# Decoder kernel: local attention's second rotation product in its own buffer and ahead of the sum of squares, with a new order of the front and cross-attention norms on ACT

## Chip, cores and metric

The kernel runs as one program on one core of a Trainium2 chip. The metric is the device time of one execution in microseconds (us). "Before" was run three times. One more execution was profiled; all times inside the kernel come from that one and count from its first instruction. Engines are called PE (matrix multiply), DVE (vector), ACT (scalar, activations), POOL (GpSimd) and SP (which here only issues DMAs).

## What is computed

The reference is a decoder of two layers, each with an attention part, a cross-attention part and a feed-forward part, on x of shape (4, 512, 128), with a layernorm behind every part. Three parts matter here.

The first part of layer 0 is a selective scan (Mamba):

```python
xn = rmsnorm(x, norm_w)
x_part, z = split(xn @ in_proj_w.T)
u = silu(conv(x_part, conv_w) + conv_b)         # causal, 4 taps
dt, Bm, Cm = split(u @ x_proj_w.T)
delta = softplus(dt @ dt_proj_w.T + dt_proj_b)
h[t] = exp(delta[t] * A) * h[t-1] + delta[t] * Bm[t] * u[t]   # 16 states
y[t] = sum(h[t] * Cm[t]) + u[t] * D
out = (y * silu(z)) @ out_proj_w.T + x
```

The second part of layer 0 is cross attention over 32 context rows with 16 heads: `xn = layernorm(x) * gamma + beta`, scores, softmax, values, an output projection, a gate `tanh(gate)`, the residual, a layernorm.

The last part of layer 1 is a local transformer of two layers (8 heads of 64, windows of 64 rows that look one window back):

```python
h = shift_token(x)
q, k, v = split(h @ wqkv)
q = l2norm(q) * q_scale ; k = l2norm(k) * k_scale
q = q * cos * scale + rotate_half(q) * sin * scale     # k likewise, with / scale
x = x + local_attention(q, k, v) @ wo
h = layernorm(shift_token(x)) * lg + lb
a, g = split(h @ w1 + b1)
x = x + (a * gelu(g)) @ w2 + b2
```

## The kernel before, in words

Everything is one program; x is kept as 16 tiles of 128 rows (4 batches of 4 tiles). Each engine runs its own instructions in the order in which the program has them. Inside a `tc.manual_schedule()` block that order is the one in which the code emits them; between such blocks the tool that builds the program may interleave. So the order on an engine is written out by hand, as lists of functions ("around", "feed", "first", "ahead", "aside").

**The front** (L355 to L400) brings batch 0 of the scan to the point where the scan can start. `squares_(b)` squares the rows of a batch on ACT and sums them on DVE into `inv`; `inverses` raises them to the power -0.5 on POOL. Batch 0 is normed, transposed (`by_features`), projected (`pi`), and convolved: half of the channels on DVE (L370, L372), the other half as matmuls with the taps multiplied into the weights (`convolved`). Two Silu on ACT give `u`. `double` computes `px` and its two copies, `xdt` in float32 and `stk` in bfloat16. `rests` and `parts` split what bfloat16 leaves over into two further bfloat16 parts of `stk` (rows 32 to 63 and 64 to 95), which the scan's matmuls broadcast. `gates` makes the gate's pre-activation, with Silu into `sz`. `steps_`, `corrected`, `reduced`, `logarithms`, `deltas`, `products` compute softplus from Abs, Relu, Exp, 1 + e, a correction, and Ln, and then `delta` and `du = delta * u`.

**The scan** (L563 to L598) has 64 steps (4 batches of 16 states). In each, `rows` broadcasts a row of B and of C by matmuls, `decay` makes `dA` on ACT (three steps ahead), `scan` multiplies `pb` by `du` and scans on DVE, and multiplies by C on POOL; `collect` sums on PE. What the next batch needs is spread over the steps ("ahead"); `gates_next` at step 5 applies Silu to `u` and `sz` of the next batch.

**Cross attention** (L971 to L1095) runs 16 tiles in two half stages, `tile_a` and `tile_b`; parts of the mixture of experts that follows are put between them ("aside"). `stats_x` takes mean and variance of a tile of the next batch (DVE) and its power -0.5 (POOL, `rpow` in `stats`). `norm_x` norms that tile on DVE (L985) and transposes it; with the batch's fourth tile ACT writes `xT`, which `score` of the next batch needs. `result` makes the residual sum r and its statistics, `norm_r` norms it on DVE (L1036).

**Local attention** (L1392 to L1866) runs 32 tiles i (2 layers of 16), each in two iterations g = 2i and 2i + 1. PSUM buffers: `pqk` (one, two banks), `psc`, `pa` (one), and `pt`, a ring of three that all transposes, `pv`, `po` and `pff` share. The functions around the change:
- `project_qk(i)`: q and k of tile i into `pqk`.
- `squares(i)`: ACT squares `pqk` into the SBUF buffer "sq", of which there is one.
- `norms(i)`: DVE sums "sq" (L1439) and takes the maximum with 1e-24 (L1440), 128x16.
- `rotated_a(i)`: DVE, `ta = pqk * cos` (L1446).
- `halves(i)`: DVE, `tb = rotate_half(pqk) * sin`, two instructions (L1453). `tb` also lies in the buffer "sq". It is the last reader of `pqk`.
- `halves_added(i)`: POOL, `ta += tb` (L1459). `lengths(i)`: POOL, power -0.5 of the sums. `scaled(i)`: POOL, `ta *= rn` (L1467).
- `turn_k(i)`, `turn_q(i)`: PE transposes of ta into `pt`; `kT` is copied by DVE (L1488), `qT` by ACT.
- `values(g)`: PE; then DVE `rc` (L1543) and `at` (L1544). `output(i)`: PE `po`, DVE `xa = po + x` (L1562).
- `ff_gates`: two of its three products are written into the `pqk` buffer, the third into `pt`. `ff_hidden`: DVE `ge` (L1614). `ff_stats`: mean and variance, four tiles at once, with a 128x4 addition (L179).

Where two tiles are in work, "around" says what is emitted when; for odd iterations:

```python
[[(turn_out, -1), (rotated_a, 3)], [(norms, 3), (rotated_b, 3)], [(project_v, 2), (output, -1)]]
```

The first tiles (0 to 2) have an order of their own ("first"), which calls norms, rotated_a, halves.

Of the kernel before, what the change touches and what calls it, by code (L numbers as in the profile page):

```python
# [19 lines left out]
P = 128  # L20
# [37 lines left out]
def decoder_kernel(ctx: ExitStack, tc: tile.TileContext, a: dict):  # L58
# [178 lines left out]
    with ExitStack() as ph:  # L237
# [77 lines left out]
            G.tensor_tensor(stk[64:96, b, :], left[64:96], mid[64:96], ALU.subtract)  # L315


        def steps_(b, c, pd):
            mm(pd, w_dt[96:104, c * P:(c + 1) * P], xdts[b][96:104])
            t = fp.tile([P, T], F32, tag="e", name="e")  # L320
            v = fp.tile([P, T], F32, tag="v", name="v")
            S.activation(t, pd, AF.Abs, bias=vcol("dt_b", c))
            S.activation(v, pd, AF.Relu, bias=vcol("dt_b", c))
            S.activation(t, t, AF.Exp, scale=-1.0)
            w = fp.tile([P, T], F32, tag="w", name="w")
            S.activation(w, t, AF.Identity, bias=1.0)
            evs[b, c] = t, v, w

        def corrected(b, c):
# [25 lines left out]
        with tc.tile_pool(name="m1ps", bufs=1, space=PSUM) as ps, tc.manual_schedule():  # L355
            squares_(0)
            inverses(0, 1)
            xns[0] = fp.tile([P, NJ, D], F32, tag="e", name="xn")
            V.tensor_tensor(xns[0], x0[:, 0:NJ, :], inv[:, 0].unsqueeze(2).to_broadcast([P, NJ, D]), ALU.mult)
            by_features(0, ps.tile([P, NJ, P], F32, tag="pt", name="pt"))  # L360
            for c in range(2):
                G.tensor_tensor(w_tap[:, c], w_tap[:, c],
                                w_in[:, c * P:(c + 1) * P].unsqueeze(1).to_broadcast([P, 4, P]), ALU.mult)
            for b in range(1, B):
                squares_(b)

# [3 lines left out]
            V.tensor_scalar(acc, pi, vcol("conv_w", 7), vcol("conv_b", 1), ALU.mult, ALU.add)  # L370
            for k in range(1, 4):
                V.scalar_tensor_tensor(acc[:, k:], pi[:, 0:T - k], vcol("conv_w", 7 - k), acc[:, k:], ALU.mult, ALU.add)  # L372
            inverses(1, B)
            pi = ps.tile([P, T], F32, tag="pi0", name="pi")
            convolved(0, 0, pi, range(4))
            S.activation(u[:, 1, 0, :], acc, AF.Silu)
            S.activation(u[:, 0, 0, :], pi, AF.Silu, bias=vcol("conv_b", 0))
            double(0, ps.tile([104, T], F32, tag="px", name="px"))
            rests(0)
            pz = [ps.tile([P, T], F32, tag=f"pz{c}", name="pz") for c in range(2)]  # L380
            for c in range(2):
                gates(0, c, pz[c])
                S.activation(sz[:, c, 0, :], pz[c], AF.Silu)
            S.activation(gate, rcol("gate"), AF.Tanh)
            pct = ps.tile([P, P], F32, tag="pi1", name="pct")
            TE.transpose(pct, ctx_sb, ident)
            V.tensor_copy(ctxT, pct)
            a0 = _VEC["A_log"][0]
            S.activation(negA, vec[:, a0:a0 + 32], AF.Exp)
            V.tensor_scalar_mul(negA, negA, -1.0)  # L390
            V.tensor_scalar_mul(gb, rcol("b_out"), gate)
            for c in range(2):
                steps_(0, c, ps.tile([P, T], F32, tag=f"pd{c}", name="pd"))
                corrected(0, c)
                reduced(0, c, (G, V)[c])
            logarithms(0)
            for c, eng in ((0, G), (1, V)):
                deltas(0, c, eng)
                products(0, c, eng)
            parts(0)  # L400


        with tc.tile_pool(name="m2", bufs=3) as t2, \
# [19 lines left out]

            def decay(k):
                b, n = steps[k]
                for c in range(2):
                    S.activation(dAs[k % 4][:, c, c:T], delta[b % 2][:, c, c:T], AF.Exp,  # L427
                                 scale=negA[:, c * NST + n:c * NST + n + 1])

# [112 lines left out]
            def gates_next(b, c):  # L542
                pi = bank()
                gates(b, c, pi)
                S.copy(sz[:, c, b, :], pi)
                if c:
                    for t in (u, sz):
                        S.activation(t[:, :, b, :], t[:, :, b, :], AF.Silu)

            def double_next(b):  # L550
                double(b, bank()[0:104])
# [417 lines left out]
            store(hf, g)  # L969

    with tc.tile_pool(name="xa", bufs=3) as t1:  # L971
        xrs, mvs, ptx, xTs, scs, mxs, xes, rcs, prs, xpTs, rs_ = ({} for _ in range(11))

        def stats_x(i):
            mvs[i] = stats(x1[:, i, :])
            xrs[i] = t1.tile([P, D], F32, tag="xr", name="xr", bufs=8)
            G.tensor_tensor(xrs[i], x1[:, i, :], gb, ALU.add)

        def norm_x(i):
            b, j = divmod(i, NJ)  # L980
            if j == 0:
                ptx[b] = ps.tile([P, NJ, P], F32, tag="ph", name="ptx")
            mv, rs = mvs.pop(i)
            xn = t1.tile([P, D], F32, tag="xn", name="xn")
            V.tensor_scalar(xn, x1[:, i, :], mv[:, 0:1], rs, ALU.subtract, ALU.mult)  # L985
            TE.transpose(ptx[b][:, j, :], xn, ident)
            if j == NJ - 1:
                xTs[b] = t1.tile([P, T], F32, tag="xT", name="xT", bufs=2)
                S.activation(xTs[b], ptx.pop(b).rearrange("p j t -> p (j t)"), AF.Identity,
                             bias=vcol("ln_b"), scale=vcol("ln_g"))  # L990

        def score(i):
            b, j = divmod(i, NJ)
# [35 lines left out]
        def result(i):  # L1029
            r = rs_[i] = t1.tile([P, D], F32, tag="r", name="r")  # L1030
            V.scalar_tensor_tensor(r, pos_.pop(i), gate, xrs.pop(i), ALU.mult, ALU.add)
            mvs["r", i] = stats(r)

        def norm_r(i):
            mv, rs = mvs.pop(("r", i))
            V.tensor_scalar(x2[:, i, :], rs_.pop(i), mv[:, 0:1], rs, ALU.subtract, ALU.mult)  # L1036

        def tile_a(k):

# [352 lines left out]
    with tc.tile_pool(name="la_b", bufs=2) as bp, tc.tile_pool(name="la_t", bufs=2) as t1, \  # L1392
# [54 lines left out]

        def halves(i):
            src = pqks.pop(i).rearrange("p w (h d) -> p w h d", d=64)
            tb = tbs[i] = t1.tile([P, 2, 8, 64], F32, tag="sq", name="tb", bufs=1)  # L1450
            for hf in range(2):
                lo = slice(32 * hf, 32 * hf + 32)
                V.tensor_tensor(  # L1453
# [13 lines left out]
            G.tensor_tensor(ta, ta, rns.pop(i).unsqueeze(2).to_broadcast([P, 16, 64]), ALU.mult)  # L1467
# [297 lines left out]
        def x_norm(b):  # L1765
# [242 lines left out]
```

## Time and profile before

| what | value |
|---|---|
| three runs | 1251.81, 1258.32, 1264.30 us; median 1258.32 |
| the profiled execution | 1261.84 us |
| its span, first to last instruction | 1260.1 us |
| granted PE clock, mean of the span | 0.942 |
| front, to the start of the first scan instruction | 38.8 us |
| last scan instruction starts | 302.1 us |
| local attention: first `pqk`, last `ptq` | 829.9 us, 1208.7 us |

How to read it: a busy share over the whole span says little, because the stages have different limits. The windows give the busy time of each engine in a stretch. In timeline lines the columns are start (us), duration (us), engine, line, operation, out<-in with shapes, count; an idle time of the engine just before the instruction stands in brackets, with what ended it. Lines of merged instructions carry "x2", "x4" and so on. A line such as "PE pff L189: 7.3, 6" below a tile's name tells that this group waited for that tile for 7.3 us in 6 waits.

### The profile page before, as it was taken

To read this page: it belongs to the slowest core of one execution; us is meant where nothing else is said; L and a number is where in the kernel's file an instruction comes from. 1 tells how busy PE (TensorE), PEld (TensorE's weight loads), DVE (VectorE), ACT (ScalarE), POOL (GpSimd) and SP (SyncE) were. 2 spreads that over 40 slices of the span, in tenths; PEclk is the share of its full clock that TensorE was granted. 3 is DMA by queue.
4 is the path that set the end of the run, shared out by engine and by line. 5 is a ranking of instruction groups with operands and counts; after the bars stand their busy time and mean duration, and the time that the engine had idled before them with its cause. 6 is when DMAs were issued, how large, how long until landed. Compare 5 with 4: busy or idle time off the path is not lost.

```text
span 1260.1 us, 22102 instructions
## 1 busy us (share of the span) xinstructions
PE 1091.9 (87%) x8377; PEld 707.5 (56%) x8377; DVE 906.1 (72%) x1720; ACT 724.6 (58%) x1608; POOL 640.4 (51%) x525
## 2 busy tenths in 40 slices
PE   4879878786788899988899999787999999999995
PEld 1334433343365789955556566455666676666664
DVE  3889898897777465847856676687787677676663
ACT  5695968662243344545556566244676666666762
POOL 4568685865445242543110100356886675676641
PEclk9799989898788898989999999789999999999997
DMA  9000000000300522200000000001111011011100
GB/s 274 1 0 1 1 0 1 0 1 25 126 1 22 191 96 84 69 29 14 2 1 2 1 2 1 1 5 23 23 27 27 18 27 27 18 27 27 27 21 28
DMA packets 38739, 39.96 MB, mean 32 GB/s; under 512 B 7544, under 2 KB 29833, under 8 KB 38153
## 3 DMA queue, kind: packets, MB, share of 16 engines
q1 hardware_dynamic: 36041, 32.73, 9.2%
q0 software_dynamic: 2048, 4.20, 1.1%
q10 hardware_dynamic: 544, 1.62, 0.4%
q8 instruction: 66, 1.08, 0.3%
q14 instruction: 40, 0.33, 0.1%
HBM read 20.80 MB, written 9.18 MB: 24 GB/s over the span
## 4 chain that ended last, share of the span: by engine, by line
PE 46%; DVE 20%; issue 3%; ACT 3%; POOL 2%; DMA 2%; DVEq 0%; ACTq 0%; SPq 0%; POOLq 0%
PE psc L189 10%; PE pqk L189 4%; PE pa L189 4%; PE ptp L1260 3%; PE phg L189 3%; PE pff L189 3%; PE po L189 3%; PE pog L189 2%; PE pv L189 2%; DVE ss L1439 2%; DVE tb L1453 2%; DVE ta L1446 2%; PE pof L189 2%; PE pq L189 1%; DMA hn<-xa 1%
## 5 line engine op out<-in xcount | busy, mean ns | idle before, releaser
L440 POOL TENSOR_TENSOR h<-h,cb 128x1024 f32<-128x1024 f32 (+1 forms) x65 | 151.8, 2338 | 65.7 <-DVE h L435 50.4
L157 POOL TENSOR_TENSOR rs<-ve,cneg 128x1 f32<-128x1 f32 (+2 forms) x83 | 59.7, 719 | 224.3 <-DVE ve L166 189.1
L435 DVE TENSOR_TENSOR_SCAN h<-dA,pb 128x1024 f32<-128x1024 f32 x64 | 146.3, 2286 | 18.4 <-ACT dA L427 4.9
L1250 ACT ACTIVATE pe<-psc,nm 128x256 f32<-128x256 f32 (+1 forms) x256 | 93.3, 448 | 74.8 <-DVE nm L1243 74.4
L189 PE MATMUL y<-h,ident 128*128 128x512 f32 x256 | 127.1, 620 | 5.5 <-POOL h L440 4.8
L1459 POOL TENSOR_TENSOR ta<-ta,tb 128x1024 f32<-128x1024 f32 x32 | 75.4, 2357 | 102.8 <-DVE rc L1543 56.6
L1243 DVE TENSOR_REDUCE nm<-psc 128x4 f32<-128x1024 f32 (+1 forms) x64 | 69.8, 1090 | 54.4 <-PE psc L189 49.1
L157 POOL TENSOR_TENSOR rn<-ss,cneg 128x16 f32<-128x16 f32 x32 | 93.0, 2905 | 0.0
L1513 DVE TENSOR_REDUCE nm<-psc 128x4 f32<-128x512 f32 x64 | 44.0, 687 | 64.2 <-PE psc L189 60.0
L427 ACT ACTIVATE dA<-delta,negA 128x512 f32<-128x512 f32 (+1 forms) x128 | 85.3, 715 | 4.7 <-POOL delta L346 4.4
L189 PEld LDWEIGHTS y<-h,ident 128*128 128x128 f32 x256 | 49.5, 197 | 65.4 <-issue 46.5
L929 ACT ACTIVATE hTg<-phg,bias 128x128 f32<-128x128 f32 x184 | 52.6, 368 | 58.0 <-PE phg L189 57.3
L432 DVE TENSOR_TENSOR pb<-du,pb 128x1024 f32<-128x1024 f32 x64 | 77.5, 1211 | 2.3 <-PE pb L189 2.2
L1522 ACT ACTIVATE pe<-psc,nm 128x128 f32<-128x128 f32 x256 | 73.6, 380 | 5.1 <-DVE nm L1513 5.0
L1260 PE MATMUL ptp<-ident,pe 128*128 128x128 f32 x448 | 66.9, 285 | 5.2 <-ACT pT L1262 2.0
L189 PE MATMUL pb<-stk,sel 96*128 96x512 bf16 x128 | 41.4, 406 | 32.7 <-DVE h L435 15.5
L189 PE MATMUL pqk<-f_qkv,hT 128*128 128x512 f32 x128 | 65.2, 633 | 5.1 <-DVE tb L1453 5.1
L189 PE MATMUL psc<-kb,qk 64*128 64x256 f32 (+1 forms) x512 | 68.0, 386 | 0.0
L1260 PEld LDWEIGHTS ptp<-ident,pe 128*128 128x128 f32 x448 | 49.4, 143 | 23.2 <-issue 8.0
L1467 POOL TENSOR_TENSOR ta<-ta,rn 128x1024 f32<-128x1024 f32 x32 | 60.9, 1902 | 2.4
L1433 ACT ACTIVATE sq<-pqk 128x1024 f32<-128x1024 f32 x32 | 32.9, 1028 | 43.9 <-PE pqk L189 40.5
L189 PEld LDWEIGHTS <-sel 96*128 96x128 bf16 x192 | 18.9, 102 | 68.9 <-issue 41.7
(382 smaller groups left out, 2853.0 us busy)
## 6 DMA issues: line engine op xcount, KB each, us to landing
vh<-va SPq DMA_DIRECT2D x56, 130.0 KB
w<-in_e_w_dram SPq DMA_DIRECT2D x16, 256.0 KB
xs<-zero SPq DMA_DIRECT2D x2, 1472.0 KB
xg<-xs SPq DMA_DIRECT2D x10, 256.0 KB
ys<-yg SPq DMA_DIRECT2D x10, 256.0 KB
f_qkv<-in_f_qkv_dram SPq DMA_DIRECT2D x1, 1536.0 KB
x<-in_x_dram SPq DMA_DIRECT2D x4, 256.0 KB
w_kv<-in_w_kv_dram SPq DMA_DIRECT2D x1, 1024.0 KB
```

Of the source, the lines that this page charges most:

```text
L157: G.tensor_tensor(out, in_, cneg.to_broadcast([P, n]), ALU.pow)
L189: TE.matmul(out, lhsT=lhsT, rhs=rhs, start=start, stop=stop)
L427: S.activation(dAs[k % 4][:, c, c:T], delta[b % 2][:, c, c:T], AF.Exp, scale=negA[:, c * NST + n:c * NST + n + 1])
L432: V.tensor_tensor(pb, du[steps[k][0] % 2], pb, ALU.mult)
L435: V.tensor_tensor_scan(h.rearrange("p c t -> p (c t)"), dAs[k % 4].rearrange("p c t -> p (c t)"), pb.rearrange("p c t -> p (c t)"), 0.0, A ...
L440: G.tensor_tensor(h[:, c], h[:, c], cb.unsqueeze(1).to_broadcast([P, n, T]), ALU.mult)
L1243: V.tensor_reduce(nm, psc[:, :, 0:nk], AX.X, ALU.max, negate=True)
L1250: S.activation(pe[:, h, 0:nk], psc[:, h, 0:nk], AF.Exp, bias=nm[:, h:h + 1])
L1260: TE.transpose(ptp[:, h * nb + kk, :], pe[:, 2 * pr + h, kk * P:(kk + 1) * P], ident)
L1459: G.tensor_tensor(ta, ta, tbs.pop(i).rearrange("p w h d -> p (w h) d"), ALU.add)
L1467: G.tensor_tensor(ta, ta, rns.pop(i).unsqueeze(2).to_broadcast([P, 16, 64]), ALU.mult)
L1522: S.activation(pes[g][:, h, :], o[:, par, q, :], AF.Exp, bias=nm[:, k:k + 1])
```

## The change

In local attention `tb` gets a buffer of its own (one, 128x1024 float32), and in the odd iterations `norms` is emitted by `rotated_b`, behind `halves` and `halves_added`, instead of ahead of them. The order of tiles 0 to 2 ("first") stays.

In the front, the sums of squares of batches 1 to 3 are moved behind the convolution, between and behind the two Silu; `rests` and `parts` are written out and put right behind `double`, with their copies on DVE instead of ACT; Relu and 1 + e of batch 0 go from ACT to DVE; the gates of batch 0 come later and are only copied, by DVE, and their Silu is applied at scan step 5 with batch 1's. The first step's decay takes c = 1 first.

In cross attention, the statistics of a batch's four tiles are kept together, with one addition and one power for the four, and with two small POOL products that make `-mean * rs`; ACT norms the four tiles (`normal`, L202) in `tile_b` of the batch's second tile, and `turn_x` transposes them in `tile_a` of the third. `result` also makes `-mean * rs` with two POOL products, and `norm_r` is done by ACT.

```diff
-        def steps_(b, c, pd):
+        def steps_(b, c, pd, eng=None):
...
-            S.activation(v, pd, AF.Relu, bias=vcol("dt_b", c))
+            if eng:
+                eng.tensor_scalar(v, pd, vcol("dt_b", c), 0.0, ALU.add, ALU.max)
+            else:
+                S.activation(v, pd, AF.Relu, bias=vcol("dt_b", c))
...
-            S.activation(w, t, AF.Identity, bias=1.0)
+            if eng:
+                eng.tensor_scalar_add(w, t, 1.0)
+            else:
+                S.activation(w, t, AF.Identity, bias=1.0)
...
-            for b in range(1, B):
-                squares_(b)
...
-            inverses(1, B)
             pi = ps.tile([P, T], F32, tag="pi0", name="pi")
             convolved(0, 0, pi, range(4))
+            squares_(1)
             S.activation(u[:, 1, 0, :], acc, AF.Silu)
             S.activation(u[:, 0, 0, :], pi, AF.Silu, bias=vcol("conv_b", 0))
+            squares_(2)
+            squares_(3)
+            inverses(1, B)
             double(0, ps.tile([104, T], F32, tag="px", name="px"))
-            rests(0)
-            pz = [ps.tile([P, T], F32, tag=f"pz{c}", name="pz") for c in range(2)]
-            for c in range(2):
-                gates(0, c, pz[c])
-                S.activation(sz[:, c, 0, :], pz[c], AF.Silu)
+            left = fp.tile([P, T], F32, tag="left", name="left", bufs=1)[0:96]
+            V.tensor_tensor(left, xdts[0][0:96], stk[:, 0, :], ALU.subtract)
+            mid = fp.tile([96, T], BF16, tag="mid", name="mid", bufs=1)
+            V.tensor_copy(mid[64:96], left[64:96])
+            V.tensor_copy(stk[32:64, 0, :], left[32:64])
+            G.tensor_tensor(stk[64:96, 0, :], left[64:96], mid[64:96], ALU.subtract)
...
             for c in range(2):
-                steps_(0, c, ps.tile([P, T], F32, tag=f"pd{c}", name="pd"))
+                steps_(0, c, ps.tile([P, T], F32, tag=f"pd{c}", name="pd"), V)
                 corrected(0, c)
                 reduced(0, c, (G, V)[c])
+            for c in range(2):
+                pz = ps.tile([P, T], F32, tag=f"pz{c}", name="pz")
+                gates(0, c, pz)
+                V.tensor_copy(sz[:, c, 0, :], pz)
             logarithms(0)
...
-            parts(0)
...
-                for c in range(2):
+                for c in range(2) if k else (1, 0):
                     S.activation(dAs[k % 4][:, c, c:T], delta[b % 2][:, c, c:T], AF.Exp,
...
-                    for t in (u, sz):
-                        S.activation(t[:, :, b, :], t[:, :, b, :], AF.Silu)
+                    for t, i in ((u, b), (sz, b)) + ((sz, 0),) * (b == 1):
+                        S.activation(t[:, :, i, :], t[:, :, i, :], AF.Silu)
...
         def stats_x(i):
-            mvs[i] = stats(x1[:, i, :])
+            b, j = divmod(i, NJ)
+            if j == 0:
+                mvs[b] = sm.tile([P, NJ, 2], F32, tag="mv4", name="mv4")
+            st = sm.tile([P, 6], F32, tag="st", name="st")
+            V.bn_stats(st, x1[:, i, :])
+            V.bn_aggr(mvs[b][:, j, :], st)
...
             if j == NJ - 1:
+                ve = sm.tile([P, NJ], F32, tag="ve4", name="ve4")
+                V.tensor_tensor(ve, mvs[b][:, :, 1], eps.to_broadcast([P, NJ]), ALU.add)
+                rs = sm.tile([P, NJ], F32, tag="rs4", name="rs4")
+                rpow(rs, ve, NJ)
+                mvs[b] = mvs[b], rs, x1[:, b * NJ:(b + 1) * NJ, :], shifts(mvs[b], rs)
+
+        def norm_x(b):
+            xns_[b] = t1.tile([P, NJ, D], F32, tag="xn", name="xn", bufs=1)
+            normal(xns_[b], *mvs.pop(b))
+
+        def turn_x(b):
+            pt = ps.tile([P, NJ, P], F32, tag="ph", name="ptx")
+            xn = xns_.pop(b)
+            for j in range(NJ):
+                TE.transpose(pt[:, j, :], xn[:, j, :], ident)
+            xTs[b] = t1.tile([P, T], F32, tag="xT", name="xT", bufs=2)
+            S.activation(xTs[b], pt.rearrange("p j t -> p (j t)"), AF.Identity, bias=vcol("ln_b"), scale=vcol("ln_g"))
...
-            mvs["r", i] = stats(r)
+            mv, rs = stats(r)
+            mr = sm.tile([P, 1], F32, tag="mr1", name="mr1")
+            G.tensor_tensor(mr, mv[:, 0:1], rs, ALU.mult)
+            G.tensor_tensor(mr, mr, cminus, ALU.mult)
+            mvs["r", i] = mr, rs
 
         def norm_r(i):
-            mv, rs = mvs.pop(("r", i))
-            V.tensor_scalar(x2[:, i, :], rs_.pop(i), mv[:, 0:1], rs, ALU.subtract, ALU.mult)
+            mr, rs = mvs.pop(("r", i))
+            S.activation(x2[:, i, :], rs_.pop(i), AF.Identity, bias=mr, scale=rs)
...
+                if k % NJ == 2:
+                    turn_x(nxt // NJ)
...
-                for j in ((), (0, 1), (2, 3), ())[k % NJ]:
-                    norm_x(nxt + j)
+                if k % NJ == 1:
+                    norm_x(nxt // NJ)
...
-            tb = tbs[i] = t1.tile([P, 2, 8, 64], F32, tag="sq", name="tb", bufs=1)
+            tb = tbs[i] = t1.tile([P, 2, 8, 64], F32, tag="tb", name="tb", bufs=1)
...
-            for f in (halves, halves_added, lengths, scaled):
+            for f in (halves, halves_added, norms, lengths, scaled):
...
-                  [[(turn_out, -1), (rotated_a, 3)], [(norms, 3), (rotated_b, 3)], [(project_v, 2), (output, -1)]]]
+                  [[(turn_out, -1), (rotated_a, 3)], [(rotated_b, 3)], [(project_v, 2), (output, -1)]]]
```

More of the change, by code (lines that the diff above doesn't have):

```diff
@@ L971, in decoder_kernel @@
     with tc.tile_pool(name="xa", bufs=3) as t1:
-        xrs, mvs, ptx, xTs, scs, mxs, xes, rcs, prs, xpTs, rs_ = ({} for _ in range(11))
+        xrs, mvs, xns_, xTs, scs, mxs, xes, rcs, prs, xpTs, rs_ = ({} for _ in range(11))
         def stats_x(i):
-            mvs[i] = stats(x1[:, i, :])
+            b, j = divmod(i, NJ)
[4 more added lines that the diff above has]
+            V.bn_aggr(mvs[b][:, j, :], st)
             xrs[i] = t1.tile([P, D], F32, tag="xr", name="xr", bufs=8)
             G.tensor_tensor(xrs[i], x1[:, i, :], gb, ALU.add)
[L979 to L986, printed above, removed]
-            if j == NJ - 1:
-                xTs[b] = t1.tile([P, T], F32, tag="xT", name="xT", bufs=2)
-                S.activation(xTs[b], ptx.pop(b).rearrange("p j t -> p (j t)"), AF.Identity,
-                             bias=vcol("ln_b"), scale=vcol("ln_g"))
+            if j == NJ - 1:
+                ve = sm.tile([P, NJ], F32, tag="ve4", name="ve4")
[13 more added lines that the diff above has]
+            S.activation(xTs[b], pt.rearrange("p j t -> p (j t)"), AF.Identity, bias=vcol("ln_b"), scale=vcol("ln_g"))
         def score(i):
```

## The prediction

> **What bounds the kernel now.** I read the page's busy table and chain first, then windows by stage, then the timelines of the three stages that the change touches.
>
> ```profile
> PE 1091.9 (87%) x8377; PEld 707.5 (56%) x8377; DVE 906.1 (72%) x1720; ACT 724.6 (58%) x1608; POOL 640.4 (51%) x525
> ...
> PE 46%; DVE 20%; issue 3%; ACT 3%; POOL 2%; DMA 2%; DVEq 0%; ACTq 0%; SPq 0%; POOLq 0%
> ```
> ```profile
> 64.00:330.00 266.00, 217.74 (x682) 102.16 (x680) 231.78 (x219) 176.13 (x315) 182.79 (x113) 0.93 0.05 18
> ...
> 960.00:1040.00 80.00, 77.91 (x821) 53.04 (x821) 57.84 (x120) 50.20 (x116) 55.21 (x31) 1.00 0.11 25
> ```
> The columns after the length are PE, PEld, DVE, ACT, POOL, then clock, DMA share, GB/s. The scan (64 to 330) belongs to DVE, 87% busy. Local attention (830 to 1230) belongs to PE, 97% busy: a wait there costs its full length. One tile of it, DVE and PE:
>
> ```profile
> 1016.58 1.21 DVE L1446 TENSOR_TENSOR ta<-pqk,tab 128x1024 f32<-128x1024 f32 x1
> 1017.71 1.21 DVE L1439 TENSOR_REDUCE ss<-sq 128x16 f32<-128x1024 f32 x1
> 1018.95 0.18 DVE L1440 TENSOR_SCALAR ss<-ss 128x16 f32<-128x16 f32 x1
> 1019.04 1.28 DVE L1453 TENSOR_TENSOR tb<-pqk,tab 128x512 f32<-128x512 f32 x2
> 1020.24 0.17 DVE L1543 RECIPROCAL rc<-pa 128x4 f32<-128x4 f32 x1
> 1020.44 0.42 DVE L1544 TENSOR_TENSOR at<-pa,rc 128x256 f32<-128x256 f32 x1
> 1020.78 0.28 DVE L1562 TENSOR_TENSOR xa<-po,x 128x128 f32<-128x128 f32 x1
> ```
> ```profile
> 1020.51 0.60 PE L1486 MATMUL ptk<-ident,ta 128*128 128x128 f32 x4
> 1021.12 0.66 PE L1477 MATMUL ptq<-ident,ta 128*128 128x128 f32 x4
> ```
> DVE works without a gap from ta to xa. `xa` reads `po`, whose PSUM buffer `ptq` takes three `pt` tiles later; xa ends at 1021.06 and ptq follows 0.06 later. Setting every xa against its next ptq weight load in the trace, 21 of 29 pairs have this distance of 0.05; the others have 0.71, 1.09, or 3.6 and more. So DVE and PE are tied in most tiles, and a DVE delay in front of xa goes straight into the time.
>
> ```profile
> 947.33 2.84 PE L189 MATMUL pff<-hnT,f_w 128*128 128x512 f32 x6 [1.22 <-DVE tb L1453]
> ```
> ```profile
>   PE pff L189: 7.3, 6
> ```
> Here PE waits for tb, which holds the `pqk` buffer: 7.3 us in six waits. This wait is what tb ahead of ss removes.
>
> ```profile
> 848.82 1.85 DVE L1440 TENSOR_SCALAR ss<-ss 128x16 f32<-128x16 f32 x1
> ```
> ```profile
> 848.73 1.90 POOL L1467 TENSOR_TENSOR ta<-ta,rn 128x1024 f32<-128x1024 f32 x1
> ```
> The reader is to see that L1440, otherwise 0.17, ran until POOL's tensor_tensor was over (850.67 and 850.63). At 926.18 it took 0.91 beside another one. The 1.21 reduce ran undisturbed beside both.
>
> **Local attention, step by step.** tb takes the place of ss at 1017.71 and ends at 1018.99. POOL's ta+=tb starts 0.14 later (as at 1009.30 after 1009.16) and lasts 2.36, to 1021.49. DVE's ss runs beside it, to 1020.12; the maximum L1440 behind it meets the POOL operation that tb has just released. In the row above the maximum lost the rest of POOL's time, so it ends at 1021.52 and rc starts at 1021.43, not 1020.24: **1.19 later**. Queued behind it on DVE are (ge,) rc, at, xa, then nm and kT; PE's ptq waits for xa. Bounds: 0 (not held) to 1.19 (held to the end); I take 1.19, since the row is the same instruction against the same kind of partner. Price: 21 x 1.19 = 25.0, plus 0.48 and 0.10 for the distances 0.71 and 1.09: +25.6. In the tiles of the pff wait xa has 3.6 to 4.6 of slack, so the delay is free there, and the 7.3 are won (tb 1.38 earlier than a wait of 1.22; next is po's end at 946.1). The separate buffer lets sq go without waiting for ta+=tb: one such wait, 3.3 at 858.8, in the start; a PE wait of 2.0 follows it, of which I take 1.5. POOL's lengths and scaled move 1.2 earlier, to nobody's gain: no PE wait is on ta. Sum: 25.6 - 7.3 - 1.5 = **+16.8**. Bounds: -8.8 without the hold, +22 if neither gain comes.
>
> The Trainium skill, "SBUF — State Buffer", section "SBUF: two separate sides", calls this pair of ports an exclusive lock: whichever of a two-port DVE operation and a GpSimd operation starts first keeps it for its whole length. The rows agree for POOL's add and multiply. They differ for its power: L1440 took 0.17 at 888.87 inside a power of 887.97 to 888.98. By the rule the front's 2.28 power would also hold DVE's left for up to 2.1 and the estimate would be some 1.5 worse; by the rows it is not.
>
> **The front.**
> ```profile
> 14.65 0.80 DVE L370 TENSOR_SCALAR u<-pi,vec 128x512 f32<-128x512 f32 x1
> ...
> 36.32 1.01 PE L189 MATMUL pb<-stk,sel 96*128 96x512 bf16 x2 [11.53 <-POOL stk L315]
> ...
> 38.76 2.29 DVE L435 TENSOR_TENSOR_SCAN h<-dA,pb 128x1024 f32<-128x1024 f32 x1
> ```
> L370 stood behind the last sum of squares (14.04); its own input was ready at 11.66. It starts 2.9 earlier, but the second Silu needs the conv matmuls (11.45 + 4.95 = 16.40, against 18.37), so px comes 1.9 earlier and stk's cast ends near 20.2. From ACT go two Silu (1.2), two Relu (1.36), two Identity (1.26), two casts (1.24); DVE gets two relu (0.80 by L370), two adds (at most 0.69), two PSUM copies (0.69), two casts (at most 0.6). DVE then carries the front: left 0.69, casts 1.2, ctxT, negA, gb 0.75, relu, add, correction twice 4.3, reduced 0.69, copies 1.38, delta and du 1.38, about 10.4 in a row: du ends near 30.6. POOL tensor_tensors beside it (1.48, 1.26, 1.26) can hold it by 0 to 3.3; before, delta took 1.40 and du 1.64 instead of 0.69 beside POOL. I take 1.5: 32.1, pb's product 1.23, scan at 33.3, **5.5 earlier**. stk is ready near 24 and no longer last. ACT's first pair of decays, now c = 1 first, waits for DVE's delta (near 31.4) and ends 1.33 later, still hidden by du and pb's product. Square between the Silus could cost two table loads of 1.28; under Exp's table Square ran without one (956.19), so I take 0. The deferred Silu of sz comes back in the scan:
> ```profile
> 74.35 2.29 DVE L435 TENSOR_TENSOR_SCAN h<-dA,pb 128x1024 f32<-128x1024 f32 x1 [3.10 <-ACT cb L422]
> ```
> ACT is full in front of this wait, and a Silu of 1.04 (row at 67.44) lengthens it: +1.0. Sum **-4.5**; bounds -6.9 (no hold, Silu hidden) to 0 (loads, all holds, Silu). SP's and POOL's DMA order is untouched.
>
> **Cross attention, 314 to 413.**
> ```profile
> 330.41 2.07 PE L189 MATMUL sc<-Gm,xT 128*128 128x512 f32 x2 [0.87 <-ACT xT L989]
> ```
> ```profile
> 331.18 1.06 DVE L1036 TENSOR_SCALAR x<-r,mv,rs 128x128 f32<-128x128 f32 x1 [0.44 <-POOL rs L157]
> ```
> At each new batch sc waits for xT. The new chain from the last statistics: power 1.03, two small POOL products 0.56, four ACT norms 1.65, transposes 0.9, xT 0.78 = 4.9. From 321.84, 342.95, 362.95 that gives 326.8, 347.9, 367.9; PE's own work ends at 327.2, 346.2, 371.3; sc stood at 330.41, 349.85, 372.61: -3.2, -2.0, -1.3 = -6.5. Of the 16 norms that leave DVE five took 1.06 beside POOL; half of the 4.6 that the chain holds of them: -2. Against it 16 x 0.56 of POOL products before xpr, 9.0 at worst; rc comes 1.6 after ve and POOL needs 1.15, so mostly hidden: +2. ACT, about 40% busy here, covers 16 norms of 0.41; if it doesn't, xpT is late next. One 128x4 addition per batch in place of four small ones (0.14) is hidden behind POOL's power. Sum **-6.5**, bounds -11 to +3.
>
> **Sum:** 16.8 - 4.5 - 6.5 = +5.8. The profiled run took 1261.84 (span 1260.1 and 1.7 around it): 1267.6. It lies 3.5 over the median of three (1258.32); for a median I predict 1264.
>
> **Rivals.**
> *No hold* (the maximum slips past POOL, or PE's slack takes it): local attention -8.8, in all -19.8: 1238. For it: L1440 is small and normally 0.17. Against: both rows beside a tensor_tensor show the hold.
> *Slower: front and cross attention give nothing.* DVE inherits the front's work and meets POOL's tensor_tensors; ACT's norms wait for POOL products ahead of xpT. From sums over 0 to +2 together it decides: 16.8 + 1 = +18, 1276. For it: the 1.06, 1.40 and 1.64 rows. Against: PE's three visible waits for xT.
> *Slower: a second collision.* POOL's scaled (1.90), now 1.2 earlier, meets the statistics' 128x4 addition at 1023.3, eight times: 8 x 1.9 = 15, 1279. Against: kT and y, queued behind it, have over 1 us of slack by the rows.
> That tb isn't earlier at all I exclude: DVE's order is written out.
>
> **How the numbers follow.** About 1% (12.6 us) is what a measurement of this kernel can tell from no change. Forecast 0.49 (1254 to 1274; 0.41 within, 0.08 slower), no hold 0.18 (0.15 faster), nothing from front and cross 0.22 (0.19 slower), second collision 0.11 (0.10 slower). Faster 0.15, same 0.48, slower 0.37. The range goes down to 1240, past no hold with half of the other gains (-8.8 - 5.5: 1244 on the median), and up to 1282, past the two slower cases; left out are about half of no hold (0.09) and the far ends of the slower ones (0.09).
>
> **What would show it.** L1440's median near 1.4, not 0.17; PE's waits for tb gone and those for xa up from 4.9 to some 25 or more; first scan near 33; sc waiting less for xT. L1440 at 0.17 beside ta+=tb would make the prediction wrong, and so would a first scan after 37.

## The result, and the profile after

| | median | runs |
|---|---|---|
| before | 1261.19 us | 12, from 1251.81 to 1265.28 |
| changed | 1265.13 us | 12, from 1260.65 to 1271.09 |

The ratio is 1.005, with a 95% interval of 1.0026 to 1.0073. Measured a second time (after_again, below), against its own runs of before, it was 1.0098 (1.0063 to 1.0132). The two intervals hardly meet: the change costs between half a per cent and one per cent, 6 to 12 us. The profiled execution of the changed kernel has a span of 1263.1 us, 3.0 more than before.

The page of the changed kernel, busy table and shares of the chain:

```profile
PE 1084.2 (86%) x8377; PEld 699.1 (55%) x8377; DVE 929.2 (74%) x1691; ACT 732.6 (58%) x1629; POOL 646.3 (51%) x554
...
PE 42%; DVE 24%; ACT 4%; issue 4%; POOL 2%; DMA 0%; DVEq 0%; ACTq 0%; POOLq 0%; SPq 0%
```
DVE has 29 instructions fewer and is busy 23.1 us longer: its instructions were stretched. Its share of the chain went from 20% to 24%. The same two windows as before:

```profile
64.00:330.00 266.00, 217.70 (x679) 102.53 (x678) 227.49 (x211) 176.04 (x318) 180.33 (x112) 0.93 0.05 18
960.00:1040.00 80.00, 73.76 (x768) 50.21 (x764) 62.57 (x111) 49.48 (x109) 49.63 (x28) 1.00 0.10 24
```
In local attention PE fell from 77.91 to 73.76 of 80 us, with DVE up from 57.84 to 62.57. The scan is hardly different. One tile of local attention, DVE first, then POOL and PE beside it:

```profile
1061.79 1.28 DVE L1480 TENSOR_TENSOR tb<-pqk,tab 128x512 f32<-128x512 f32 x2
1062.99 1.21 DVE L1466 TENSOR_REDUCE ss<-sq 128x16 f32<-128x1024 f32 x1
1064.23 1.37 DVE L1467 TENSOR_SCALAR ss<-ss 128x16 f32<-128x16 f32 x1
1065.52 0.17 DVE L1570 RECIPROCAL rc<-pa 128x4 f32<-128x4 f32 x1
1065.72 0.42 DVE L1571 TENSOR_TENSOR at<-pa,rc 128x256 f32<-128x256 f32 x1
1066.06 0.28 DVE L1589 TENSOR_TENSOR xa<-po,y 128x128 f32<-128x128 f32 x1
```
```profile
1063.21 2.36 POOL L1486 TENSOR_TENSOR ta<-ta,tb 128x1024 f32<-128x1024 f32 x1 [3.71 <-DVE tb L1480]
```
```profile
1066.40 0.66 PE L1504 MATMUL ptq<-ident,ta 128*128 128x128 f32 x4 [1.21 <-DVE xa L1589]
```
tb releases POOL's addition, which runs from 1063.21 to 1065.57. The reduce passes beside it in its usual 1.21. The maximum (now L1467), 0.17 when alone, starts inside the addition and ends at 1065.60, with it. rc, at and xa stand behind it on DVE, and PE's ptq waits 1.21 us for xa. Over all 32 tiles, and PE's ptq waiting for xa (us and times), in the changed kernel and then in the kernel before:

```profile
L1467 DVE TENSOR_SCALAR ss<-ss x32: 175/1372/1385, 823.6 to 1200.3; 128x16 f32<-128x16 f32 x32
```
```profile
  PEld ptq L1504: 23.3, 21
...
  PE ptq L1504: 18.2, 15
```
```profile
  PEld ptq L1477: 4.9, 15
```
The waits of ptq's weight load rose from 4.9 us in 15 to 23.3 in 21; those of its matmul lie mostly at the same time and are not added. PE's six waits of pff for tb are gone from the list. From one fourth tile to the next takes 49.65 us instead of 47.36 (xa's ends, 1004.99 to 1054.64, against 1010.56 to 1057.92).

The front's DVE, from the stretch that the prediction listed:

```profile
12.11 0.81 DVE L374 TENSOR_SCALAR u<-pi,vec 128x512 f32<-128x512 f32 x1 [4.06 <-PE pi L189]
...
20.21 0.69 DVE L387 TENSOR_TENSOR left<-xdt,stk 96x512 f32<-96x512 f32 x1 [0.33 <-ACT stk L304]
...
27.00 1.64 DVE L348 TENSOR_TENSOR v<-v,e 128x512 f32<-128x512 f32 x1
...
32.63 2.29 DVE L446 TENSOR_TENSOR_SCAN h<-dA,pb 128x1024 f32<-128x1024 f32 x1
```
```profile
19.96 2.28 POOL L157 TENSOR_TENSOR inv<-inv,cneg 128x12 f32<-128x12 f32 x1 [8.39 <-DVE inv L276]
```
The first scan starts 6.13 us earlier. L348, 0.69 before, is one instruction that met a POOL operation. `left` took its usual 0.69 in the middle of POOL's power, which ran from 19.96 to 22.24: it was not held.

### The profile page after: what moved, and what is told of

Same layout as the page of the kernel before. It is cut to its first block, busy times and chain, and to the rows that moved or that the text cites. A ratio compares the mean times of both kernels' runs of the same rounds, so it can differ in the third digit from the quotient of the medians.

```text
span 1263.1 us, 22137 instructions
## 1 busy us (share of the span) xinstructions
PE 1084.2 (86%) x8377; PEld 699.1 (55%) x8377; DVE 929.2 (74%) x1691; ACT 732.6 (58%) x1629; POOL 646.3 (51%) x554
## 4 chain that ended last, share of the span: by engine, by line
PE 42%; DVE 24%; ACT 4%; issue 4%; POOL 2%; DMA 0%; DVEq 0%; ACTq 0%; POOLq 0%; SPq 0%
PE psc L189 9%; PE pqk L189 4%; PE pa L189 4%; PE ptp L1287 3%; PE po L189 3%; PE pff L189 3%; PE phg L189 3%; DVE ss L1467 3%; PE pog L189 2%; DVE tb L1480 2%; DVE ss L1466 2%; DVE ta L1473 2%; PE pof L189 2%; DVE nm L1540 1%; PE pq L189 1%
## 5 line engine op out<-in xcount | busy, mean ns | idle before, releaser
L157 POOL TENSOR_TENSOR rs<-ve,cneg 128x1 f32<-128x1 f32 (+2 forms) x74 | 56.3, 760 | 214.7 <-DVE ve L166 176.6
L438 ACT ACTIVATE dA<-delta,negA 128x511 f32<-128x511 f32 (+1 forms) x128 | 85.3, 715 | 6.3 <-POOL delta L352 4.4
L189 PE MATMUL phg<-xgT,wt 128*128 128x128 f32 x368 | 51.1, 282 | 4.7 <-DVE wt L932 4.5
```

What stands on the lines that cost most here:

```text
L157: G.tensor_tensor(out, in_, cneg.to_broadcast([P, n]), ALU.pow)
L189: TE.matmul(out, lhsT=lhsT, rhs=rhs, start=start, stop=stop)
```

## The experiments

Each kernel was compared with the kernel before on its own chip, so ratios can be compared, and single times across chips less well. First all of them in one table. The milestones are starts in the profile in us: the first scan, the first score product of cross attention (sc), the first product of the experts (phg), local attention's first pqk; LA is the time from that pqk to the end of the span.

| kernel | ratio (95%) | scan | sc | phg | pqk | LA |
|---|---|---|---|---|---|---|
| before | 1 | 38.76 | 314.02 | 423.18 | 829.93 | 430.17 |
| changed | 1.005 (1.0026–1.0073) | 32.63 | 312.61 | 418.71 | 817.01 | 446.09 |
| after_again | 1.0098 (1.0063–1.0132) | 32.65 | 313.84 | 422.31 | 833.71 | 446.96 |
| la_undone | 0.9943 (0.9921–0.9964) | 33.55 | 315.12 | 420.90 | 837.13 | 428.07 |
| la_alone | 1.015 (1.0126–1.0174) | 38.92 | 314.40 | 423.72 | 834.36 | 447.10 |
| no_max | 0.9852 (0.9827–0.9878) | 33.00 | 314.33 | 419.35 | 831.05 | 415.63 |
| max_on_pool | 0.9848 (0.9819–0.9877) | 32.25 | 312.01 | 418.10 | 830.13 | 415.39 |
| front_alone | 1.0011 (0.9994–1.0028) | 32.46 | 312.60 | 420.13 | 827.23 | 426.37 |
| cross_alone | 0.9995 (0.9968–1.0021) | 40.26 | 316.13 | 422.32 | 827.74 | 428.26 |
| early_unit | 1.0102 (1.0077–1.0127) | 33.20 | 310.76 | 416.83 | 824.62 | 446.92 |
| pool_max_and_early_unit | 0.9848 (0.9819–0.9877) | 31.97 | 313.71 | 420.94 | 825.53 | 415.90 |
| own_buffer_only | 0.9967 (0.9944–0.9991) | 32.86 | 314.08 | 419.10 | 830.79 | 429.63 |
| old_order_pool_max | 0.9905 (0.9869–0.9941) | 32.65 | 312.77 | 418.73 | 833.93 | 422.25 |
| la_alone_pool_max | 0.9905 (0.9869–0.9940) | 41.23 | 315.28 | 422.63 | 836.33 | 415.46 |

The theory: the loss lies in local attention alone, in one DVE instruction, the maximum, which the new order puts next to the POOL addition. The rivals: it is the buffer, or the longer queue, or POOL's earlier operations; or front and cross attention lose something.

### la_undone and la_alone: the parts apart

la_undone is the changed kernel with local attention as before:

```diff
-            tb = tbs[i] = t1.tile([P, 2, 8, 64], F32, tag="tb", name="tb", bufs=1)
+            tb = tbs[i] = t1.tile([P, 2, 8, 64], F32, tag="sq", name="tb", bufs=1)
...
-            for f in (halves, halves_added, norms, lengths, scaled):
+            for f in (halves, halves_added, lengths, scaled):
...
-                  [[(turn_out, -1), (rotated_a, 3)], [(rotated_b, 3)], [(project_v, 2), (output, -1)]]]
+                  [[(turn_out, -1), (rotated_a, 3)], [(norms, 3), (rotated_b, 3)], [(project_v, 2), (output, -1)]]]
```
la_alone is before with the reverse of this and nothing else.

> The front and cross-attention parts of the change stay, local attention is as before. By the theory (the maximum held by POOL costs local attention 25 us, the earlier tb and the own buffer win about 9) the time is 16 us below the changed kernel's 1265: about 1249, 12 below before; the stage up to the first pqk takes 817 as in the changed kernel. By the rival (local attention's loss comes from how the stage is entered, from the earlier parts) the stage from the first pqk to the end stays at 446 and the time near 1263.

> Only the local-attention part of the change on the kernel before. Theory: first pqk at 830 as before, the stage 16 us longer, about 1277 against 1261; L1440 (here another line number) at a median of 1.37 us. Rival: the stage is as long as before (430) and the time stays at 1261.

Measured 0.9943 and 1.015. LA is 428.07 without the part and 447.10 with it: the loss is in local attention, some 17 us, whatever front is ahead of it. The two ratios add up to +0.93%, between the two measurements of the whole. Two forecasts for la_undone missed: it is 0.57% below before, about 7 us and not 12, and its first pqk comes at 837.13, not at 817 (see after_again).

### no_max and max_on_pool: take away the held instruction

no_max is the changed kernel without the maximum; the clamp of the sums at 1e-24 is left out of the computation. max_on_pool lets POOL take it, right ahead of its power:

```diff
-            V.tensor_scalar_max(ss, ss, 1e-24)
...
-            rpow(rns[i], sss.pop(i), 16)
+            ss = sss.pop(i)
+            G.tensor_scalar_max(ss, ss, 1e-24)
+            rpow(rns[i], ss, 16)
```

> The changed kernel without the maximum of the sums with 1e-24 (this clamp is left out of the computation; nothing else is). Theory of the hold: rc follows the sum at once, PE's waits of ptq for xa fall from 41 us to under 8, local attention gets 25 to 27 us shorter: about 1239. Rival (the delay is the order of sum and tb, or POOL's earlier ta+=tb, not the held maximum): only 32 x 0.09 = 3 us, about 1262.

> The changed kernel with the maximum as a POOL instruction in front of the power, behind ta+=tb in POOL's own order. Theory of the hold: as without a maximum, DVE goes from the sum straight to rc; POOL has 0.2 to 0.3 us more per tile in a stage where it is 65% busy: 1239 to 1241, 20 below before. Rival: 1262; or POOL's chain is late and turn_k waits for ta, 32 x 0.3 = 10 us of the gain lost.

Measured 0.9852 and 0.9848; LA 415.63 and 415.39, 30 to 31 us below the changed kernel. The same DVE stretch and POOL's new instruction in max_on_pool:

```profile
1069.47 1.21 DVE L1466 TENSOR_REDUCE ss<-sq 128x16 f32<-128x1024 f32 x1
1070.60 0.17 DVE L1571 RECIPROCAL rc<-pa 128x4 f32<-128x4 f32 x1
1070.81 0.42 DVE L1572 TENSOR_TENSOR at<-pa,rc 128x256 f32<-128x256 f32 x1
1071.15 0.28 DVE L1590 TENSOR_TENSOR xa<-po,y 128x128 f32<-128x128 f32 x1
```
```profile
1072.03 0.26 POOL L1490 TENSOR_SCALAR ss<-ss 128x16 f32<-128x16 f32 x1
```
```profile
960.00:1040.00 80.00, 79.33 (x840) 54.27 (x840) 57.05 (x112) 53.26 (x118) 59.33 (x40) 1.00 0.11 25
```
rc starts 1.13 after the reduce, not 2.53; nothing waits for POOL's 0.26; PE is busy 79.33 of 80 us. The addition on POOL and the reduce on DVE run beside each other as before, so it is neither the order nor the addition by itself that costs: it is the small instruction that meets it. This version beats both kernels.

### own_buffer_only and old_order_pool_max: order and buffer apart

Both keep tb's own buffer and go back to the order of before; the second also has the maximum on POOL.

```diff
-            for f in (halves, halves_added, norms, lengths, scaled):
+            for f in (halves, halves_added, lengths, scaled):
...
-                  [[(turn_out, -1), (rotated_a, 3)], [(rotated_b, 3)], [(project_v, 2), (output, -1)]]]
+                  [[(turn_out, -1), (rotated_a, 3)], [(norms, 3), (rotated_b, 3)], [(project_v, 2), (output, -1)]]]
```

> After, with the order of before in the odd iterations (norms ahead of rotated_b); tb keeps its own buffer. My theory: the loss of local attention lies in the order, that puts the maximum L1440 next to the POOL addition that tb releases, and the buffer is worth only one wait in the start (1.5 us). Then the time from the first pqk to the end is about 427 (428.1 with neither buffer nor order, 446.1 with both), the maximum's median is 174 ns, and the ratio to before is 0.993 (0.990 to 0.997). Rival: the separate buffer itself changes the timing (sq written earlier, ACT and POOL shifted) and carries part of the loss: 435 to 446 and a ratio of 1.00 to 1.005.

> After, with the order of before (norms ahead of rotated_b) and the maximum done by POOL in front of its power. Theory: tb ahead of ss is itself worth the wait of pff for tb (7.3 in six waits), so that this kernel, which gets rid of the maximum but not of that wait, lies between: the maximum off DVE brings 0.1 us in front of xa in some 21 tiles (about -2), the buffer 1.5, so 424 to 425 from the first pqk to the end, ratio 0.991. Rival: the order is worth nothing by itself, and the 415 of the kernel with the order and the maximum on POOL came from the maximum's leaving DVE: then 415 to 417 here too, ratio 0.985.

Measured 0.9967 and 0.9905. With the old order the maximum is short again, though tb keeps its own buffer (own_buffer_only):

```profile
L1467 DVE TENSOR_SCALAR ss<-ss x32: 174/174/908, 837.3 to 1196.1; 128x16 f32<-128x16 f32 x32
```
So the loss belongs to the order, not to the buffer, and the buffer alone shows no gain (429.63 against 428.07). LA now stands in a square:

| LA, us | maximum on DVE | maximum on POOL |
|---|---|---|
| old order | 429.63 | 422.25 |
| new order | 446.09, 446.96 | 415.39 |

Down the right column the order alone gains 6.9, with one profile at the upper end (the ratios, 0.9905 and 0.9848, differ by about as much). It fits the wait of pff for tb, which is still there in old_order_pool_max and gone in max_on_pool:

```profile
  PEld pff L189: 7.2, 6
  PE pff L189: 6.1, 6
```
The maximum costs 7.4 in the old order and 31.1 in the new: 23.7 are the collision's. With the 426.4 to 430.2 that the old order shows in its five profiles with the maximum on DVE, it is 23 to 27. The 7.4 were expected at about 2, a miss: without the maximum tb starts 1.13 after the reduce instead of 1.33, so it is 0.20 in each tile, not 0.1, and the one collision that own_buffer_only had (0.91) goes as well. In some 21 tiles that is about 5 us; the rest lies within the scatter of the old order. From one fourth tile to the next takes 47.37, 46.65, 49.65 and 45.52 us in the four kernels of the square (own_buffer_only, old_order_pool_max, changed, max_on_pool).

### front_alone, cross_alone, la_alone_pool_max: what the other parts bring

front_alone and cross_alone are before with only the front's, and only cross attention's, part of the diff. la_alone_pool_max is before with local attention's part and the maximum on POOL.

> Only the front's part of the change on the kernel before. The first scan starts at 33, 6 earlier than before; by the theory (the first steps of the scan are tied to PE, whose convolution for the next batch starts no earlier than ACT lets it, and the deferred Silu lengthens ACT's full stretch) 4 to 5 of them are given back before the 17th scan, which starts 1 to 2 earlier than before (103.0): the time is 1 to 3 below before. Rival (the front's gain lasts, less 1 for the Silu, as predicted): 17th scan near 98, time 4.5 below.

> Only the cross-attention part on the kernel before. Up to the fourth batch's first maximum 3 to 4 us are won (3.2 + 2.0 + 1.3 predicted at the three new batches), as in the changed kernel; by the theory they shrink to 1 to 3 at the first product of the experts, because the routing's DVE chain and ACT's norms behind POOL's products take over: time 2 to 3 below before. Rival (as predicted): 6.5 below.

> Before, with the local attention's part of the change alone (own buffer, new order) and the maximum on POOL; front and cross attention as before. Theory: front and cross attention are worth 0.57% together (from the kernel without the local attention part), so local attention 415 to 417 and a ratio of 0.991, 0.6% above the kernel with everything and the maximum on POOL (0.9848). Rival: front and cross attention are worth nothing that lasts (each alone measured 1.0011 and 0.9995), so a ratio of 0.985 to 0.987.

Measured 1.0011, 0.9995 and 0.9905. Each alone brings nothing that can be measured: for the time, a miss for both. In front_alone's profile the 17th scan starts at 101.46, 1.6 earlier than before, as its theory said. Together they bring 0.57% by la_undone, and as much by the distance from la_alone_pool_max (0.9905) to max_on_pool (0.9848). A third reading is smaller: own_buffer_only, which has both parts and the old order, is 0.33% below before. With intervals of about 0.2 to 0.4% on each ratio, and the kernels on different chips, 0.3 to 0.6% is what the record supports; that the two parts need each other is not shown. In the profiles of the table, the eight kernels with the new front (without the two of early_unit) reach sc at 313.4 in the mean, the four with the old front at 315.0: -1.5, of the -7.0 by which the first scan of the eight is earlier in the mean. From sc to phg the eight kernels with the new cross attention (again without the two of early_unit) take 106.1 in the mean, the four with the old one 108.3: -2.3. That is 3.8 of the 4 to 7 us that the ratios give; where a rest would come from is open.

The front's gain is lost in two places. The fourth to seventh and the tenth scan instruction of the changed kernel:

```profile
44.28 2.29 DVE L446 TENSOR_TENSOR_SCAN h<-dA,pb 128x1024 f32<-128x1024 f32 x1 [0.87 <-PE y L189]
...
48.37 2.29 DVE L446 TENSOR_TENSOR_SCAN h<-dA,pb 128x1024 f32<-128x1024 f32 x1 [0.67 <-ACT cb L433]
...
52.45 2.29 DVE L446 TENSOR_TENSOR_SCAN h<-dA,pb 128x1024 f32<-128x1024 f32 x1 [0.68 <-PE y L189]
...
56.53 2.29 DVE L446 TENSOR_TENSOR_SCAN h<-dA,pb 128x1024 f32<-128x1024 f32 x1 [0.68 <-ACT cb L433]
...
72.31 2.29 DVE L446 TENSOR_TENSOR_SCAN h<-dA,pb 128x1024 f32<-128x1024 f32 x1 [4.87 <-PE y L189]
```
The fifth to seventh now come 4.08 us after the one ahead, PE's time for one step with the next batch's convolution in it; before, DVE's 3.5 us ruled up to the fifth. By the ninth scan (64.04 against 67.75) 2.4 of the 6.1 are gone, by the tenth (72.31 against 74.35) another 1.7. The second loss is dearer than the Silu of 1.0 that was moved there:

```profile
63.31 1.99 ACT L559 ACTIVATE sz<-sz 128x1024 f32<-128x1024 f32 x2
```
```profile
68.45 0.58 PE L189 MATMUL pc<-stk,sel 96*128 96x512 bf16 x1 [2.60 <-ACT cb L433]
68.84 3.27 PE L189 MATMUL y<-h,ident 128*128 128x512 f32 x4
```
The same two in the kernel before:

```profile
71.63 0.38 PE L189 MATMUL pc<-stk,sel 96*128 96x512 bf16 x1 [1.65 <-ACT cb L422]
71.85 1.88 PE L189 MATMUL y<-h,ident 128*128 128x512 f32 x4
```
And two windows of the changed kernel:

```profile
68.00:70.00 2.00, 1.54 (x3) 0.93 (x3) 0.00 (x0) 2.00 (x5) 1.52 (x1) 0.55 0.00 0
70.00:72.00 2.00, 2.00 (x3) 0.36 (x2) 0.00 (x0) 1.07 (x2) 0.84 (x1) 0.59 0.00 0
```
ACT is full, cb comes later, PE stands idle for 2.60 us instead of 1.65, and then its granted clock is 0.55 to 0.59, so the four y products take 3.27 instead of the 1.88 that they took before behind the idle time of 1.65, with the clock at 1.00. In all ten kernels with the new front the clock of the 3.6 us behind the gap was 0.53 to 0.62, in all four with the old front 1.00. The Trainium skill, "TensorE: Matmul & The Clock Gate", section "Part 1: The HAM clock gate (the "warmup" mystery)", says that the clock halves after an idle window of about 3.4 us; here 2.60 us of idleness were enough, behind a stretch (64 to 68) with PE busy 1.86 of 4 us.

### early_unit and pool_max_and_early_unit: an attempt to keep the front's gain

ACT's part of the next batch (`unit(1)`) is put ahead of the first decays, so that PE gets its convolution work sooner:

```diff
-                for k in range(3):
-                    decay(k)
-                for k in range(2):
-                    rows(k)
                 unit(1)
+                decay(0)
+                rows(0)
                 turn_next(1)
+                decay(1)
+                decay(2)
+                rows(1)
```

> The changed kernel with the norms of batch 1 ahead of the first decay on ACT and its transposes behind the first rows on PE. Theory (PE's late start of the next batch's convolution takes the front's gain back): the 17th scan starts 2 to 3 us earlier than in the changed kernel (101.4), near 99, and the time falls by as much, to 1262.5 where the changed kernel has 1265. Rival (only the deferred Silu, or the scan's own DVE work, takes it back): 17th scan at 101.4 and no change.

> Both amendments on the changed kernel: the maximum on POOL and the early norms of batch 1. If both theories hold the gains add: 19 below before for the first and 2 to 3 for the second, 21 to 22 below before, ratio 0.983. If the second is nothing, 0.985 as with the maximum on POOL alone.

Measured 1.0102 and 0.9848. In early_unit's profile the waits of the fourth to sixth scan are gone and the ninth scan starts 29.0 after the first (31.4 in the changed kernel, 29.0 before), as intended; in the other kernel the waits begin again at the fifth. In early_unit the 17th scan starts at 99.62, 1.8 earlier than in the changed kernel (expected near 99); in the other it starts at 102.70. The times show nothing of it: 1.0102 stands beside 1.0098 and 1.005, and 0.9848 beside 0.9848. No gain is shown; one of 1.8 us (0.14%) would be too small for these ratios to show.

### after_again

> The changed kernel once more, next to these on the same chip, for its place in the sums. If the parts add up (local attention alone 1.015, the rest 0.9943), its ratio is 1.009; the first measurement gave 1.005 (1.003 to 1.007). My theory, that the stages are nearly independent, expects 1.005 to 1.010. In its profile the time from the first pqk to the end is 446 again, while the unchanged stage from the experts' first product to the first pqk (398 in the first profile, 405 to 416 in the other kernels) is again anywhere between 398 and 416; were it 398 again, the change would have a part in that stage after all, which I don't expect.

The changed kernel unaltered: ratio 1.0098, LA 446.96, from phg to pqk 411.4 us instead of 398.3. That stage is the same code in all kernels, and took 398 to 416 in the profiles. So most of the 12.9 us by which the first profile reached pqk early were not the change's. Much of the spread goes with the chip: the four profiles of one chip (front_alone, cross_alone, and the two of early_unit) took 404.6 to 407.8 in this stage, the four of a second (la_undone, la_alone, no_max, max_on_pool) 410.6 to 416.2, the other four, among them after_again, 411.4 to 415.2. The granted clock can be a part of it; the stretch from 540 to 600 in the changed kernel's first profile and in after_again's (not the same work: they hold 527 and 377 matmuls):

```profile
540.00:600.00 60.00, 54.42 (x527) 35.37 (x530) 40.82 (x88) 34.34 (x90) 25.00 (x29) 1.00 0.07 19
```
```profile
540.00:600.00 60.00, 49.40 (x377) 29.74 (x378) 32.84 (x64) 25.59 (x68) 24.60 (x27) 0.89 0.10 26
```
Over the whole stage the clock was 0.97 and 0.96, which is worth about 4 of the 13.1 us at most, and own_buffer_only, with 0.97 too, took 411.7. What else makes the difference is open, and what sets the clock there was not tried.

## Why the prediction was right, and where it was not

The predicted time, 1264, and "within 1%" came true by the first measurement; the second puts the change at the edge of 1%. The steps, in their own order:

- **The hold: right.** The maximum took 1.30 to 1.39 in 29 of the 32 tiles (tiles 0 to 2 keep their old order), forecast "near 1.4". Predicted +25.6; the square shows 23.7, or 23 to 27 with its scatter. The waits of ptq's weight load for xa were forecast at "some 25 or more" and came to 23.3.
- **tb ahead of ss wins the pff wait: right.** Predicted -7.3, shown -6.9 (old_order_pool_max to max_on_pool).
- **A row and a bound that do not carry what they were given for.** That POOL's power does not hold the maximum was read from L1440 at 888.87; but that power ends at 888.98 and L1440 at 889.04, so it could have been held to the end. The reading itself is right: another pair of rows of the kernel before shows it, and so does `left` in the changed kernel, for which the prediction took no hold:

```profile
936.07 0.17 DVE L1440 TENSOR_SCALAR ss<-ss 128x16 f32<-128x16 f32 x1
```
```profile
935.59 1.01 POOL L157 TENSOR_TENSOR rs<-ve,cneg 128x4 f32<-128x4 f32 x1
```
  The upper bound for local attention "if neither gain comes" should be +25.6, the hold alone, and not +22.
- **The separate buffer, -1.5: not confirmed**, LA is 429.63 with it and 428.07 without (own_buffer_only, la_undone), within the scatter of the old order.
- **Local attention in all:** predicted +16.8; 15.9 between the two first profiles, 16.9 from before to la_alone, 19.0 from la_undone to la_alone, and 18.9 by la_alone's ratio. What the change was about was understood; the term for the buffer was small enough not to matter.
- **The front, "5.5 earlier": right at the first scan** (33.3 forecast, 32.6 measured); the casts took 0.42 each and Square brought no table load; `left` was not held by the power. **What lasts of it was mis-sized:** "+1.0" for the deferred Silu left out that PE, idle for 2.60 us, comes back at half its clock (1.4 on y), and that the fourth to seventh step would run at PE's pace (2.4). Predicted -4.5, in the profiles -1.5.
- **Cross attention, -6.5: mis-sized.** Score 5 came 2.8 earlier (327.63 against 330.41, forecast 3.2), but 1.4 of that lay in the earlier start of the stage; by the ninth tile 3.5 us were won (maximum of the scores at 347.04 against 351.96, less the 1.4 at the start). At the sixteenth they were nearly all given back (387.20 against 389.00). Which wait took over was not tried. In the list of this stage (314 to 413) the longest is DVE's for the output projection, 5.3 us in 7 in the kernel before, and a new one is that of the ACT norm for its two POOL products (in us, times, longest):

```profile
DVE r L1052 <- PE po L189: 21.2, 8, 9.5
ACT x L1061 <- POOL mr L1056: 15.3, 7, 5.4
```
  A further 2.7 is won between there and phg. Predicted -6.5, in the profiles -2.3. The rival "front and cross attention give nothing" was nearer to the truth than the chance of 0.22 says: each alone gives nothing that can be measured, both together 0.3 to 0.6%.
- **No hold and the second collision: not seen.** The hold decided. The statistics' addition (L179) took 0.163 in the median in local attention and 0.808 at the longest, as before (0.161 and 0.806): it met nothing new.
- **The sum** was helped. With the sizes of the profiles it would have been about 16.4 - 1.5 - 2.3 = +12.6, which is what after_again shows (1.0098, 12.4 us); the first measurement gave 1.005. The two terms, together -11, were too large, and the first measurement lies on the low side of the two: that the time came out as close as 1264 against 1265.13 was partly luck.

## What to carry to other kernels

Before an instruction on DVE is moved, look at what the instruction ahead of it releases on POOL: here a long one moved forward was worth 6.9 us, and a maximum of 0.17 us, left right behind the release, cost 23.7. The cure was to keep the new order and give the small instruction to POOL, in front of its own power, where nobody waits for its 0.26 us: 1.5% below the kernel before. A gain at one point of a pipeline goes into the sum only when it has been followed to the end of its stage, past the engine that rules there next.

## What the runs showed of the hardware that was not expected

- PE's granted clock fell to 0.53 to 0.62 (mean of the next 3.6 us) behind an idle time of 2.60 us and stayed at 1.00 behind one of 1.65, at the same place of the scan, in ten and four profiles. So idle time of an engine that is not the bottleneck did cost something: 1.4 us on the next products. The length of one idle time is not the whole rule: in the kernel before the clock fell behind one of 2.13 (at 92.7), and in four kernels with the new front (after_again, la_undone, no_max, own_buffer_only) also behind one of 1.68 or 1.69, just ahead of the 17th scan, which then starts at 102.93 to 103.81 (101.44 in the changed kernel). In the traces the clock changes only after multiples of some 3.4 us. In the scans of the fourteen profiles PE had been busy for 1.34 us or less in the 3.4 us ahead of 56 of the 60 falls, and for 1.72 or 1.73 ahead of those four; behind no 3.4 us with so little work did it stay at 1.00, and between 1.40 and 1.73 it did both.
- POOL's power does not hold DVE's small instructions: 0.17 for the maximum inside a power of 1.01 (936.07, before), 0.18 inside one of 2.91 (846.68, changed), 0.69 for `left` inside one of 2.28. POOL's addition holds the maximum to its end, in the new order in 29 of the 32 tiles. A reduce of 1.21 beside the same addition isn't touched.
- The stage from phg to pqk, with the same code and the same data, took 398 to 416 us in fourteen profiles, and 3 to 6 us of spread were left among the four of one chip. So one pair of profiles can't carry a difference of 10 us in it; comparing the stage that was changed (LA within about 1 us for the kernels with the new order, within 4 for those with the old one) could.
